# A recurrence whose backward numerator scan runs over pairs of tokens

## The chip, the cores and the metric

The kernel runs on one core of a Trainium2 chip. A core has five engines that each take their instructions in order from a queue of their own: PE (matrix products), DVE (vector operations and scans), ACT (functions of one input), POOL (a second, slower vector engine) and SP, which here only starts transfers. They wait for each other by semaphores. [...] The metric is the device time of one execution in microseconds. The kernel before takes 1098.87 us, the median of 3 runs (1096.25 to 1105.0).

## The reference

Two layers follow each other. The first is a linear attention over 1024 tokens, 1024 channels and 4 batches, run in both directions; the second is a slot attention, which the change leaves alone. The first, cut to what matters:

```
decay = exp(-exp(w)) * (0.5 + 0.5*tf)          # per batch and channel
ek  = exp(min(kf, 30)); ekv = ek * vf          # here k and v are one input
a_t = a_{t-1}*decay + ekv_t                    # forward: nf, df
...                                            # the same backward: nb, db
euk = exp(min(u + kf, 30))
num = nf + nb - ekv + euk*vf
den = df + db - ek + euk
out = sigmoid(r) * (num / max(den, 1e-8)) * (0.8 + 0.2*tf)
```

## The kernel before

Channels lie on the 128 partitions, tokens along the free axis. The recurrence is a loop of 32 passes, one for each batch and block of 128 channels, each over a tile of 128 x 1024. Pass i's numbers are written here as i modulo 4, since four passes share one load of r (`gate`) and one sigmoid over it (L279).

A forward scan followed by a backward scan over its result gives nf + nb - ekv, up to a factor that is put into the inputs. So each pass needs four scans on DVE: forward over `ek` and `ekv`, and backward over each result in place (`scan`, L320). The tile `both` holds denominator and numerator side by side; there are two such tiles, used in turn. The first value of a backward scan (the edge) is made by ACT (`make_edge`, L332).

The order of the work is written out by hand: nearly every instruction is pinned to program order. In pass i DVE runs the two forward scans and the backward scan of the denominator (in `sums_a`), then `den_sum` (L360, adds the own term), `newton` (L419) of pass i-1, `own_value` (L364) and the backward scan of the numerator (`numerator`). Beside it:

- POOL runs `gated` of pass i-1 (L412, L413), `terms` of pass i+1 (L302, L308), `floor` (L381, after `den_sum`) and `product` of pass i-1 (L431, after `newton`). `product` reads the tile `both` of pass i-1, which is also the one that the forward scans of pass i+1 write: they wait for it.
- ACT runs the exponentials (L312, L292), the logarithm and exponential of the quotient (`guess`, L397 and L399), a square (L434), the two edges, and the copies out of the PSUM tile `ptr` (L457, L489, L504).
- PE sums the numerator in PSUM with the sign turned: `add_negated` (L370) multiplies by minus the identity, first the own values `ov`, later the scanned numerator, 2 products each. It also contracts gates and squares for the routing logits (`contract`, L442) and turns pass i-2's tokens in two halves (`turn_half`, L456).

Three passes in four turn tokens in this place (i modulo 4 = 1, 2, 3). From pass 3 on these also do one piece of weight work (`projection`, L488 or L496). In i modulo 4 = 1 and 2 a further half is turned at the end of the pass and copied in the next. All of these share one buffer `ptr`: each use waits until ACT has copied the one before. Passes with i modulo 4 = 0 turn nothing and do no weight work. The PE order of pass i is: first half turned, `contract` of a square, second half turned, `contract`, the weight piece, `add_negated` of `ov`, `contract` of gates of pass i-1, the further half, `add_negated` of the numerator.

The last pass works in halves, and its last steps lie on the way to the top-8 search that opens the second layer.

## Time and profile before

| quantity | us |
|---|---|
| median of 3 runs | 1098.87 |
| profiled execution, whole time | 1097.41 |
| its span, first to last instruction | 1095.6 |
| start of the first and of the last `den_sum` (L360) | 18.6 and 405.9 |
| DVE busy from 38 to 406 us | 366.48 of 368.00 |
| POOL busy in the same stretch | 338.73 |
| PE busy in the same stretch | 300.06 |
| ACT busy in the same stretch | 255.12 |

Mean granted TensorE clock over the span: 0.962. The profile cuts the span into 40 slices of about 27.4 us; the recurrence fills the first 15 of them. In the profile, a line of the timeline gives the start of an instruction or of a row of equal ones, how long it took, its engine, its line in the code, its output and inputs, and in brackets how long the engine had been idle before it and who ended that.

### The profile page before, as it was taken

How to read it: one execution, taken by the hardware profiler on the slowest of the kernel's cores; microseconds unless marked ns; L12 is line 12 of the kernel's file. 1: busy time of each engine (PE TensorE's matmuls, PEld its weight loads, DVE VectorE, ACT ScalarE, POOL GpSimd, SP SyncE). 2: the span in 40 equal slices, each digit the busy share in tenths (PEclk: the TensorE clock that was granted, in tenths of full speed). 3: DMA queues.
4: the chain of work that ended last, by engine and by line, in shares of the span. 5: the costliest groups of instructions: out<-in, count | busy, mean ns of one | idle time of the engine just before them, and what ended most of it. 6: DMA issues, size and time to landing. Idle time of an engine off the chain costs nothing.

```text
span 1095.6 us, 11962 instructions
## 1 busy us (share of the span) xinstructions
PE 972.7 (89%) x4156; PEld 541.9 (49%) x4156; DVE 767.0 (70%) x1049; ACT 507.5 (46%) x787; POOL 546.4 (50%) x417
## 2 busy tenths in 40 slices
PE   2688788877878788899999999998999999999996
PEld 0123222222323233584666666664584676766763
DVE  7999999999999995144666666656144555555555
ACT  5476777768676763012334444444123333333332
POOL 4999999999999882100222222222100444434444
PEclk9789899989989899999999999999999999999999
DMA  8575574856564265790577777553760454545554
GB/s 272 181 261 170 155 225 128 281 153 232 171 212 129 82 200 156 256 355 16 203 277 281 267 253 273 205 200 120 282 260 20 149 216 179 213 188 208 192 210 154
DMA packets 121788, 218.79 MB, mean 200 GB/s; under 512 B 10928, under 2 KB 76592, under 8 KB 121728
## 3 DMA queue, kind: packets, MB, share of 16 engines
q1 hardware_dynamic: 87872, 199.15, 51.3%
q10 hardware_dynamic: 33280, 16.78, 5.3%
q0 software_dynamic: 576, 2.10, 0.5%
q8 instruction: 33, 0.54, 0.2%
q14 instruction: 27, 0.22, 0.1%
HBM read 150.90 MB, written 67.11 MB: 199 GB/s over the span
## 4 chain that ended last, share of the span: by engine, by line
PE 58%; DVE 31%; issue 4%; POOL 3%; ACT 2%; DMA 1%; SPq 0%; POOLq 0%; DVEq 0%; ACTq 0%
DVE both L320 22%; PE psc L1095 20%; PE po L1152 19%; DVE both L419 3%; DVE ov L364 3%; PE ptr L1083 3%; PE pk L955 3%; PE pkv L885 3%; PE pv L1023 2%; PE pet L1141 1%; PE pw L835 1%; PE raw L442 1%; PE poc L1168 1%; PE num L370 1%; PE pmix L817 1%
## 5 line engine op out<-in xcount | busy, mean ns | idle before, releaser
L1095 PE MATMUL psc<-km,xt 128*128 128x272 f32 (+1 forms) x1024 | 238.4, 386 | 0.0
L1152 PE MATMUL po<-vm,e 128*128 128x512 f32 x512 | 230.4, 593 | 0.9 <-ACT e L1142 0.9
L1095 PEld LDWEIGHTS psc<-km,xt 128*128 128x128 f32 x1024 | 189.5, 190 | 29.1
L370 PE MATMUL num<-ov,minus_ident 128*128 128x512 f32 x128 | 88.6, 831 | 97.6 <-DVE ov L364 97.6
L1129 POOL TENSOR_TENSOR e<-e,den 128x256 f32<-128x256 f32 x64 | 40.5, 633 | 252.5 <-DVE den L1127 231.4
L320 DVE TENSOR_TENSOR_SCAN both<-columns,edges,both 128x1024 f32<-128x1024 f32 x64 | 148.2, 2316 | 0.0
L1152 PEld LDWEIGHTS po<-vm,e 128*128 128x128 f32 x512 | 94.8, 190 | 95.7 <-issue 85.4
L1193 DVE SCALAR_TENSOR_TENSOR y<-y,inv,npost_bc 128x1024 f32<-128x1024 f32 x62 | 79.6, 1285 | 41.2 <-POOL inv L1188 41.2
L1161 DVE TENSOR_TENSOR y<-po,y 128x512 f32<-128x512 f32 x128 | 85.8, 674 | 30.9 <-PE po L1152 30.6
L1181 ACT ACTIVATE junk<-y 128x1024 f32<-128x1024 f32 x63 | 66.7, 1058 | 69.2 <-DVE y L1193 69.1
L370 PEld LDWEIGHTS num<-ov,minus_ident 128*128 128x128 f32 x128 | 28.2, 244 | 134.3 <-issue 67.7
L1188 POOL TENSOR_TENSOR inv<-mean,minus_half 128x1 f32<-128x1 f32 x64 | 35.5, 555 | 96.8 <-DVE mean L1186 96.8
L412 POOL TENSOR_TENSOR both<-both,quo 128x1024 f32<-128x1024 f32 (+1 forms) x33 | 75.7, 2295 | 14.9 <-ACT quo L399 14.0
L308 POOL TENSOR_TENSOR ekv<-ek,kf 128x1024 f32<-128x1024 f32 (+1 forms) x33 | 75.6, 2293 | 2.6
L1142 ACT COPY e<-pet 128x256 f32<-128x256 f32 x64 | 23.8, 371 | 113.1 <-PE pet L1141 112.9
L413 POOL TENSOR_TENSOR gate<-gate,quo 128x1024 f32<-128x1024 f32 (+1 forms) x33 | 75.3, 2283 | 0.0
L431 POOL TENSOR_TENSOR gate<-gate,both 128x1024 f32<-128x1024 f32 x31 | 73.3, 2366 | 1.2
L1290 POOL TENSOR_TENSOR y<-y,xin 128x1024 f32<-128x1024 f32 x31 | 73.1, 2358 | 1.4 <-DVE y L1193 1.4
L320 DVE TENSOR_TENSOR_SCAN both<-columns,ek 128x1024 f32<-128x1024 f32 (+1 forms) x32 | 71.5, 2234 | 2.0 <-POOL gate L431 2.0
L320 DVE TENSOR_TENSOR_SCAN both<-columns,ekv 128x1024 f32<-128x1024 f32 (+1 forms) x32 | 71.4, 2231 | 0.0
L442 PE MATMUL raw<-gate,lhs 128*32 128x512 f32 x128 | 69.3, 666 | 0.6 <-POOL gate L431 0.5
L1186 DVE TENSOR_SCALAR mean<-total 128x1 f32<-128x1 f32 x64 | 9.8, 153 | 85.1 <-ACT junk L1181 45.7
(203 smaller groups left out, 1536.9 us busy)
## 6 DMA issues: line engine op xcount, KB each, us to landing
y<-rows SPq DMA_DIRECT2D x64, 512.0 KB, 4.2
kf<-in_ft_dram SPq DMA_DIRECT2D x32, 512.0 KB, 5.3
gate<-in_xt_dram SPq DMA_DIRECT2D x32, 512.0 KB, 6.5
turned_rows<-gate SPq DMA_DIRECT2D x32, 512.0 KB, 3.5
xt<-turned_rows SPq DMA_DIRECT2D x32, 512.0 KB, 5.2
rows<-y SPq DMA_DIRECT2D x32, 512.0 KB, 2.9
xin<-in_x_dram SPq DMA_DIRECT2D x32, 512.0 KB, 4.5
rows<-stage ACTq DMA_DIRECT2D x31, 512.0 KB, 4.4
```

Of the source, the lines that this page charges most:

```text
L308: pin(nc.gpsimd.tensor_tensor(ekv[:, part], ek[:, part], kf[:, part], ALU.mult))
L320: nc.vector.tensor_tensor_scan(dst[:, way], dec, src[:, way], start, ALU.mult, ALU.add)
L370: nc.tensor.matmul(num_ps[:, ts(h, 512)], minus_ident, src[:, ts(h, 512)], start=first, stop=not first,)
L412: pin(nc.gpsimd.tensor_tensor(den, den, quo[:, part], ALU.mult))
L413: pin(nc.gpsimd.tensor_tensor(xk, xk, quo[:, part], ALU.mult))
L431: pin(engine.tensor_tensor(xk, xk, factor[:, part], ALU.mult))
L442: nc.tensor.matmul(raw[rows_b, ts(h, 512)], lhs[:, w].rearrange("p h s -> p (h s)"), src[:, ts(h, 512)], start=(k == 0 and w == k), stop=( ...
L1095: nc.tensor.matmul(psc[g][:, :n], xt_g[g][:, k, :], maps["km"][:, g // NT, k, :n], start=(k == 0), stop=(k == NK - 1),)
L1152: nc.tensor.matmul(po, et[:, ts(c, P)], vm[:, c, ts(h, 512)], start=(c == 0), stop=(c == 1),)
L1161: pin(nc.vector.tensor_add(half, po, half))
L1193: pin(nc.vector.scalar_tensor_tensor(y[g], y[g], inv[g], npost_bc, ALU.mult, ALU.mult))
L1290: pin(nc.gpsimd.tensor_add(y[g - 1], y[g - 1], xin[g - 1]))
```

## The change

The numerator's backward scan runs over 512 pairs where it ran over 1024 tokens. With f the forward result and d the decay, PE makes the pairs f[2s] + d*f[2s+1] in PSUM (2 products, one by a diagonal matrix of d, one by the identity), DVE scans them backward with d*d and writes the even tokens into `both` in place, and PE makes the odd tokens: f[2s+1] + d*y[2s+2]. The own values are written by DVE straight into the PSUM tile `num`, even tokens first, odd ones behind; PE adds three products to it (even tokens, odd f, d times the next even one). The sign is no longer turned; `newton` subtracts the other way round. The pairs use the buffer `ptr`. ACT makes the diagonal matrix of d in each pass. The last pass keeps its backward scan over all tokens, and adds it to `num` in the plain order. The PE order of pass i becomes: first half turned, `contract`, second half turned, `contract`, the weight piece, `make_pairs`, `contract` of gates of pass i-1, the further half, `add_pairs`.

```
-            edge = edges[:, i % 8, :]
+            flat = rec.tile([P, 2 * L + 2], F32, tag="both", bufs=2, name=f"both_{i}")
+            both = flat[:, : 2 * L].rearrange("p (n t) -> p n t", n=2)
+            edge = [edges[:, i % 8, :], flat[:, 2 * L : 2 * L + 1]]
...
+        def parted(tokens, i):
+            return tokens.rearrange("p (s h) -> p h s", h=2) if i < N - 1 else by_half(tokens)
+
+        def by_half(tokens):
+            return tokens.rearrange("p (h s) -> p h s", h=2)
+
         def own_value(i, kf, own):
-            ov = rec.tile([P, L], F32, tag="ov", bufs=1, name=f"ov_{i}")
-            pin(nc.vector.scalar_tensor_tensor(ov, own, EXP_CLAMP, kf, ALU.min, ALU.mult))
-            return ov
-
-        def add_negated(num_ps, src, first, halves=(0, 1)):
...
+            num_ps = rec_ps.tile([P, L], F32, tag="num", bufs=1, name=f"num_{i}")
+            pin(
+                nc.vector.scalar_tensor_tensor(
+                    by_half(num_ps), parted(own, i), EXP_CLAMP, parted(kf, i), ALU.min, ALU.mult
+                )
+            )
+            return num_ps
+
+        def add(num_ps, h, src, by=ident):
+            pin(
+                nc.tensor.matmul(
+                    num_ps[:, ts(h, 512)], by, src, start=False, stop=True, skip_group_check=True
+                )
+            )
...
+        def decay_matrix(i):
+            m = rec.tile([P, P], F32, tag="decay_matrix", bufs=2, name=f"decay_matrix_{i}")
+            pin(nc.scalar.mul(m, ident, decay[:, i // NK, i % NK : i % NK + 1]))
+            return m
+
+        def make_pairs(i, both, by):
+            f = both[:, 1, :].rearrange("p (s h) -> p h s", h=2)
+            pairs = rec_ps.tile([P, 4, P], F32, tag="ptr", bufs=1, name=f"pairs_{i}")
+            pairs = pairs.rearrange("p q c -> p (q c)")
+            pin(nc.tensor.matmul(pairs, by, f[:, 1], start=True, stop=False))
+            pin(nc.tensor.matmul(pairs, ident, f[:, 0], start=False, stop=True))
+            return pairs
+
+        def add_pairs(num_ps, flat, by):
+            f = flat[:, L : 2 * L].rearrange("p (s h) -> p h s", h=2)
+            later = flat[:, L + 2 :].rearrange("p (s h) -> p h s", h=2)[:, 0]
+            add(num_ps, 0, f[:, 0])
+            add(num_ps, 1, f[:, 1])
+            add(num_ps, 1, later, by)
...
-        def numerator(i, both, edge):
-            num = both[:, 1, :]
-            scan(num, num, i, edge[:, 1:2], True)
+        def numerator(i, both, edge, pairs):
+            even = both[:, 1, :].rearrange("p (s h) -> p h s", h=2)[:, 0]
+            dec = decay_2[:, i // NK, i % NK : i % NK + 1].to_broadcast([P, L // 2])
+            pin(
+                nc.vector.tensor_tensor_scan(
+                    even[:, ::-1], dec, pairs[:, ::-1], edge, ALU.mult, ALU.add
+                )
+            )
...
+            if i < N - 1:
+                pairs[i] = make_pairs(i, both[i], by[i])
             if past:
                 gated(i - 1, both[i - 1], quo[i - 1])
...
-            ov = own_value(i, kf[i], own[i])
-            num_ps[i] = rec_ps.tile([P, L], F32, tag="num", bufs=1, name=f"num_{i}")
-            add_negated(num_ps[i], ov, True)
+            num_ps[i] = own_value(i, kf[i], own[i])
             if i == N - 1:
                 break
-            numerator(i, both[i], edge[i])
+            numerator(i, both[i], edge[i], pairs[i])
...
             if past:
                 square(i - 1, quo[i - 1])
+            if i + 1 < N - 1:
+                by[i + 1] = decay_matrix(i + 1)
+            if past:
                 contract(i - 1, gate_of(i - 1), (i - 1) % NK)
...
-            add_negated(num_ps[i], both[i][:, 1, :], False)
+            add_pairs(num_ps[i], flat[i], by[i])
```

More of the change, by code (lines that the diff above doesn't have):

```diff
@@ L228 @@
     plus_half = rc.tile([P, 1], F32, name="plus_half")
-    minus_ident = rc.tile([P, P], F32, name="minus_ident")
+    decay_2 = rc.tile([P, B, NK], F32, name="decay_2")
     nc.scalar.activation(w_sb, w_sb, AF.Exp)
@@ L246 @@
     nc.vector.tensor_scalar_mul(twice_root, twice_root, 2.0)
-    nc.vector.tensor_scalar_mul(minus_ident, ident, -1.0)
     dec_flat = decay.rearrange("p b k -> p (b k)")
+    nc.vector.tensor_tensor(decay_2.rearrange("p b k -> p (b k)"), dec_flat, dec_flat, ALU.mult)
     gap = rc.tile([P, B * NK], F32, name="gap")
@@ L262 @@
         dec_ps = columns[:, : B * NK].rearrange("p (b k) -> p b k", k=NK)
-        edges = rc.tile([P, 8, 2], F32, name="edges")
+        edges = rc.tile([P, 8, 1], F32, name="edges")
         nc.vector.tensor_copy(dec_ps, decay)
@@ L327, in sums_a @@
             b, k = i // NK, i % NK
-            both = rec.tile([P, 2, L], F32, tag="both", bufs=2, name=f"both_{i}")
-            edge = edges[:, i % 8, :]
+            flat = rec.tile([P, 2 * L + 2], F32, tag="both", bufs=2, name=f"both_{i}")
+            both = flat[:, : 2 * L].rearrange("p (n t) -> p n t", n=2)
+            edge = [edges[:, i % 8, :], flat[:, 2 * L : 2 * L + 1]]
             def make_edge(n):
-                pin(nc.scalar.mul(edge[:, n : n + 1], both[:, n, L - 1 : L], turn[:, b, k : k + 1]))
+                pin(nc.scalar.mul(edge[n], both[:, n, L - 1 : L], turn[:, b, k : k + 1]))
             late = i % HK == 1
@@ L354, in sums_a @@
             den = both[:, 0, :]
-            scan(den, den, i, edge[:, 0:1], True)
-            return both, edge
+            scan(den, den, i, edge[0], True)
+            return both, edge[1], flat
         def den_sum(both, own):
@@ L365, in own_value @@
-            return ov
-        def add_negated(num_ps, src, first, halves=(0, 1)):
-            for h in halves:
-                pin(
-                    nc.tensor.matmul(
-                        num_ps[:, ts(h, 512)],
-                        minus_ident,
-                        src[:, ts(h, 512)],
-                        start=first,
-                        stop=not first,
-                    )
-                )
+            num_ps = rec_ps.tile([P, L], F32, tag="num", bufs=1, name=f"num_{i}")
@@ L381, in floor @@
             pin(nc.gpsimd.tensor_scalar(den, den, DEN_MAX, DEN_MIN, ALU.min, ALU.max))
-        def numerator(i, both, edge):
-            num = both[:, 1, :]
-            scan(num, num, i, edge[:, 1:2], True)
+        def numerator(i, both, edge, pairs):
[6 more added lines that the diff above has]
+            )
         def numerator_half(i, both, edge, h):
             num = both[:, 1, ts(h, 512)]
-            scan(num, num, i, edge[:, 1:2] if h else both[:, 1, 512:513], True)
+            scan(num, num, i, edge if h else both[:, 1, 512:513], True)
         def guess(i, both, parts=(every,)):
@@ L417, in newton @@
             b = i // NK
+            den = both[:, 0, part]
+            num = num_ps[:, part]
+            if out is None:
+                den, num = parted(den, i), by_half(num)
             pin(
                 nc.vector.scalar_tensor_tensor(
-                    both[:, 0, part] if out is None else out[:, part],
-                    both[:, 0, part],
+                    den if out is None else out[:, part],
+                    den,
                     twice_root[:, b : b + 1],
-                    num_ps[:, part],
+                    num,
                     ALU.subtract,
                     ALU.mult,
+                    reverse0=True,
                 )
@@ L524 @@
         ek, ekv, both, edge, own, quo, num_ps = {}, {}, {}, {}, {}, {}, {}
+        flat, pairs, by = {}, {}, {}
         halves = [ts(0, 512), ts(1, 512)]
@@ L532 @@
         ekv[0] = terms(0, kf[0], ek[0], halves)
+        num_ps[0] = rec_ps.tile([P, L], F32, tag="num", bufs=1, name="num")
+        for h in range(2):
+            nc.tensor.matmul(
+                num_ps[0][:, ts(h, 512)], ident, logits[:, ts(h, 512)], start=True, stop=True
+            )
+        by[0] = decay_matrix(0)
         late_copy = None
@@ L540 @@
             own[i] = rec_ps.tile([P, L], F32, tag="own", bufs=1, name=f"own_{i}")
-            both[i], edge[i] = sums_a(
+            both[i], edge[i], flat[i] = sums_a(
                 i,
@@ L636 @@
             gated(i, both[i], quo[i], part)
-            add_negated(num_ps[i], both[i][:, 1, :], False, (h,))
+            add(num_ps[i], h, both[i][:, 1, part])
             if n == 0:
@@ L698 @@
                 pin(nc.tensor.transpose(banks[n][:, q, :], block, ident))
-        stage_last = rec.tile([P, 2, L], F32, tag="both", bufs=2, name="stage_last")[:, 0, :]
+        stage_last = rec.tile([P, 2 * L + 2], F32, tag="both", bufs=2, name="stage_last")[:, :L]
         stage_last = stage_last.rearrange("p (t c) -> p t c", c=P)
```

## The prediction

> **What bounds the kernel now.** I read the busy slices of the page first, then the chain that ended last, then the timeline of one period. In the slices, DVE is full in the first 15:

> ```profile
> DVE  7999999999999995144666666656144555555555
> POOL 4999999999999882100222222222100444434444
> PEclk9789899989989899999999999999999999999999
> ```

> The chain in order of time agrees: it runs through DVE scans, one piece of four for each pass, 12.44 to 12.52 us apart:

> ```profile
> 147.75 8.87 DVE both L320 x4
> 160.20 8.87 DVE both L320 x4
> 172.64 8.87 DVE both L320 x4
> ```

> From the first `den_sum` at 18.6 to the last at 405.9 the 31 periods average 12.49. The timeline of the period from 152 shows what the other engines have to spare:

> ```profile
> 152.11 2.26 DVE L320 TENSOR_TENSOR_SCAN both<-columns,ekv 128x1024 f32<-128x1024 f32 x1
> 153.92 0.60 PE L456 MATMUL ptr<-ident,gate 128*128 128x128 f32 x4
> ...
> 154.41 0.29 ACT L332 ACTIVATE edges<-both,turn 128x1 f32<-128x1 f32 x1 [0.97 <-DVE both L320]
> ...
> 157.68 0.58 ACT L489 COPY wp<-pwt 128x512 f32<-128x512 f32 x1 [0.97 <-PE pwt L488]
> 157.79 1.27 DVE L419 SCALAR_TENSOR_TENSOR both<-both,twice_root,num 128x1024 f32<-128x1024 f32 x1
> ...
> 159.15 2.37 POOL L431 TENSOR_TENSOR gate<-gate,both 128x1024 f32<-128x1024 f32 x1
> ...
> 160.11 2.34 DVE L320 TENSOR_TENSOR_SCAN both<-columns,edges,both 128x1024 f32<-128x1024 f32 x1
> ...
> 160.25 3.45 PE L370 MATMUL num<-ov,minus_ident 128*128 128x512 f32 x4 [2.61 <-DVE ov L364]
> ```

> To be seen: DVE never pauses; the buffer `ptr` is free again at 158.26, only 1.85 before the numerator's scan at 160.11; POOL needs 11.63 for its six steps (L412 starts at 149.90 and at 161.53, no pause between); PE stands still before L370, and then its four records take 3.45 where 1.98 is usual.

> **DVE's own work.** From 160.11 to 172.56 the starts give 2.26 + 2.18 + 2.18 + 2.36 for the scans, then 1.14, 1.19, 1.14: 12.45. The numerator's scan falls to 512 elements; the one row of such a backward scan is 1283 ns, less the 0.09 by which DVE's instructions overlap: 1.20, so -1.06. `own_value` now writes the tile that `newton` just read and must wait for its end: 1.30 in place of 1.19, +0.11. Writing PSUM costs 756 ns in the 512-wide L419 of the last pass, against 692 in L671 of the same shape into SBUF: +0.07. DVE would need 12.45 - 1.06 + 0.18 = 11.57. With nothing else late, 31 periods give 27 us.

> The pairs come from PSUM, which no scan's data did; the 1283 ns row already reads its decay there, and I keep 1.20 (bounds 1.20 to 1.35, 0 to 5 us in all). `own_value`, `newton` and the scan now step over every second element. No row does. Their contiguous forms cost 1.14 to 1.20, and doubled they would add 1.1 each. [...] `own` lies in PSUM. [...]

> ACT's new diagonal matrix is like the 128x128 copy of L514, 0.27 us. It stands after the square, ahead of the next edge, for which ACT waits 0.29 to 1.31 in the rows of L332; ACT has 113 of 368 us idle. Nothing; uncovered it is 8 us. `decay_2` and two zeroing products before the loop hide in PE's and DVE's waits for the first loads. No transfer is added or moved on SP, ACT or POOL.

> **POOL's handover.** `product` frees the tile that the next forward scan writes. From the start of `newton`: 1.27, 2.37 and two hand-overs of 0.04 are 3.72; DVE's own way is 1.30 + 1.21 + 1.20 = 3.71. Just even. POOL's 11.63 is a floor of its own, 0.06 above DVE.

> **The new wait: pairs.** The numerator's scan now waits for `make_pairs`, and the next three DVE scans and `den_sum` are queued behind it; POOL's `floor` waits for those. Let E be the end of the forward scan over `ekv`. DVE comes to the numerator at E + 5.74 now (154.37 to 160.11), after at E + 5.92. PE's chain in a turning pass, from the start of its first half, by the rows from 153.92: ACT's last copy out of `ptr` ends 4.34 later (158.26). Then two 512-wide products, 0.955 apart (1.91), and 0.15 for the last one's end and the hand-overs: 6.40.

> When does that first half start? Call N the start of the numerator's scan in the pass before and s the time it was late. `newton` ends 1.24 before N - s, so `product` ends at N + 1.17 - s. PE waits for it, then contracts gates (1.83), turns the further half if there is one (0.58), and adds three products (2.87, one more than now): N + 5.87 - s, or 6.45 - s. E is N + 5.65. So the scan is late by s' = 0.70 - s, or 1.28 - s, and never under 0.1, as ACT cannot copy before the edge at E + 0.3. For i modulo 4 = 1, 2, 3 (the further half lies before 2 and 3): 0.70, 0.58, 0.70. In the fourth pass the pairs are ready at N + 9 against 11.57: none. Four periods are 4 x 11.57 + 1.98 + 0.1 (POOL) = 48.36 against 49.8; 7.75 such groups give -11.2. The four passes with the longer weight piece (1.17 for 0.65, with a copy of 0.37 for 0.58) give +1.3. So -9.9 at full PE clock.

> **The clock.** In the pass without turning, PE is done at N + 9, and has nothing until `product` ends at N + 12.8: idle for 3.8. Before, it stands still here too (2.6 to 5.0), but then only added to a tile that nobody needed for 9 us. The stretches from 115 to 170 show what follows (columns: PE, PEld, DVE, ACT, POOL busy, then the granted clock):

> ```profile
> 118.90:122.20 3.30, 0.00 (x0) 0.00 (x0) 3.27 (x4) 3.27 (x4) 3.00 (x3) 1.00 0.00 0
> 122.30:125.70 3.40, 2.76 (x4) 1.18 (x4) 3.40 (x3) 3.37 (x4) 3.39 (x2) 0.50 0.20 53
> 125.80:129.10 3.30, 3.30 (x5) 0.53 (x4) 3.30 (x2) 1.46 (x3) 3.30 (x3) 0.50 0.96 256
> 156.40:159.80 3.40, 1.24 (x6) 0.42 (x4) 3.37 (x4) 1.54 (x3) 3.37 (x3) 1.00 1.01 370
> 159.80:163.20 3.40, 2.95 (x4) 1.17 (x4) 3.40 (x3) 3.37 (x4) 3.38 (x2) 0.51 1.10 356
> ```

> A stretch of 3.4 us with PE busy for only 1.24 is followed by half clock; one with 2.76 of 3.40 does not end it. [...] By the rows, 1.24 us of work do not save a window, and nearly every such pass goes to half clock. [...] Half clock then lasts 2.9 to 6.3 us of the work that follows (one or two windows, less what lies in the idle time), of which half is lost: 1.5 to 3.1, middle 2.3. That work is the contraction, the three products and the first turned half, straight ahead of the pairs of i modulo 4 = 1. So s = 0.70 + 2.3 = 3.0 there; in the next pass PE has room (0.1), then 1.28 - 0.1 = 1.2: 4.3 for 2.0. Seven groups: +16.1.

> **The end.** In the last pass two products of `ov` at half clock (3.44 us at 409.46) stood on the chain; they are gone, but the first half scan ends at 410.6 and PE still has its two others to do: -1.5.

> **The sum.** -9.9 + 16.1 - 1.5 = +4.7. The profiled execution took 1097.41 (span 1095.6): 1102.1. The median is 1.5 above that execution: 1104.

> **The rivals.** (A) Faster: PE keeps its clock, or its lateness is absorbed. For it: PE stood still for 2.2 us before 147.81 and for 1.5 before 185.21 and kept its clock. Against: 3.8 is longer than both, and 2.6 before 160.25 lost it. -11.4 in all, 1087; and were the pairs never late at all, 27 us and 1072. (B) Slower, by one mechanism: half clock lasts three windows, up to the pairs of the pass after. Place: i modulo 4 = 1, seven times. It decides once the window behind the first has PE busy for under some 2.8 of 3.4; the waits on `ptr` leave such holes. Three windows are 10.2, half lost 5.1 in place of 2.3: 2.8 x 7 = +20, so 1124. For it: two windows at 122.3 in the trace. Against: the three added products fill the second window. (C) Slower: the step of two in PSUM doubles `own_value`: 1138.

> **How the numbers follow.** Chances: forecast 0.43, A 0.22, B 0.25, C 0.10. The forecast's own range is 1098 to 1111 (0.8 us of lost clock either way times seven, and 1 to 2 for the scan's bounds). The range from 1085 to 1125 cuts off half of A and most of C. A change of 1% (11 us) is about what a measurement of this kernel can tell from none. Faster: 0.17 of A. Slower: B, C and 0.04 of the forecast, 0.39. Within: 0.44.

> **What would show it.** The numerator's scan at about 1.28 and its start late on PE's pairs, by about 3 us every fourth pass; periods of 11.6 elsewhere; half clock at each i modulo 4 = 0. Wrong, if no stall stands before that scan, if it is near 2.3, or if `own_value` or `newton` grow by half a microsecond.

## The result, and the profile after

The changed kernel takes 1106.68 us (median of 20 runs, 1103.21 to 1113.58), the kernel before 1098.24 (20 runs, 1095.6 to 1105.0): ratio 1.0079, 95% interval 1.0061 to 1.0097. It is slower by 0.8%. The forecast was 1104, within 1%.

The profiled execution has a span of 1107.1 us, 11.5 more than before. Of these, 9.55 lie in the recurrence (first to last `den_sum`: 18.04 to 414.86, 396.82 for 387.27), which began 0.56 earlier. From the last `den_sum` to the first copy of the raw logits the time is 14.98 for 15.24. The other 2.7 lie in the second layer, which the change leaves alone: in this execution a stretch of half clock from 454.3 to 461.1 falls on it, and 2.64 of the 2.7 arise between 456 and 466. Such stretches lie elsewhere in other executions (from 436.2 on in e10, at 437.9 and 492.5 in e1), so the medians' 8.4 is the better size.

The same three rows of the page's slices, for the kernel after:

```profile
DVE  7898898989898986233666656565233555555555
POOL 4999898989898972200222222222100343444444
PEclk9899898989899899899999999999999999999999
```

DVE was full in nearly each of the first 15 slices; now every second one has a hole. The granted clock dips in about every second slice too. The timeline of DVE in a quiet pass and the pass after it:

```profile
224.51 1.23 DVE L374 SCALAR_TENSOR_TENSOR num<-own,kf 128x1024 f32<-128x1024 f32 x1
225.65 1.27 DVE L417 TENSOR_TENSOR_SCAN both<-decay,both,pairs 128x512 f32<-128x512 f32 x1
226.96 2.29 DVE L320 TENSOR_TENSOR_SCAN both<-columns,ek 128x1024 f32<-128x1024 f32 x1
...
234.91 1.27 DVE L458 SCALAR_TENSOR_TENSOR both<-both,twice_root,num 128x1024 f32<-128x1024 f32 x1
236.22 1.23 DVE L374 SCALAR_TENSOR_TENSOR num<-own,kf 128x1024 f32<-128x1024 f32 x1
240.80 1.28 DVE L417 TENSOR_TENSOR_SCAN both<-decay,both,pairs 128x512 f32<-128x512 f32 x1 [3.35 <-ACT quo L434]
```

The scan is 1.27 for 2.34, `own_value` 1.23, and the quiet pass (numerator of i modulo 4 = 0, at 225.65) has no hole. In i modulo 4 = 1 DVE stands still for 3.35. The bracket names ACT's L434, but the chain of waits in order of time gives the true releaser, PE's pairs:

```profile
226.97 3.62 PE raw L482 x4
230.60 3.79 PE num L382 x6
234.39 0.44 PE ptr L496 x4
...
238.62 1.17 PE pairs L398 x2
239.79 0.92 PE pairs L399 x2
240.71 0.03 issue
240.73 0.02 DVEq L417
240.75 0.05 issue
240.80 1.28 DVE both L417
```

So the path to the end leaves DVE and runs through PE, with one copy on ACT in between, for nearly 14 us. Four stretches of the windows view around it (columns as in the prediction: PE, PEld, DVE, ACT, POOL busy, then the granted clock, DMA share, GB/s) show why the two first steps take 3.62 and 3.79:

```profile
222.20:225.60 3.40, 0.54 (x2) 0.00 (x0) 3.37 (x3) 3.29 (x4) 2.41 (x3) 1.00 0.01 2
225.60:229.00 3.40, 2.02 (x3) 0.54 (x4) 3.37 (x3) 3.37 (x5) 3.39 (x2) 0.50 0.29 95
229.00:232.40 3.40, 3.40 (x5) 0.83 (x3) 3.40 (x3) 1.66 (x4) 3.40 (x3) 0.50 0.72 214
232.40:235.80 3.40, 3.40 (x12) 1.29 (x11) 3.30 (x3) 0.59 (x1) 3.32 (x3) 1.00 0.00 0
```

PE has 0.54 us of work in the first stretch, and the next two are granted half the clock: 6.83 us. That is two windows of 3.413: within the span, each stretch of half clock in this trace is one or two of these long. This repeats: between 100 and 400 us half clock begins at 123.2, 174.4, 225.6, 276.8, 328.0 and 379.2, once in four passes, and lasts 6.83 each time (in the group before these it begins at 75.4 and lasts 3.41). The periods (from one `den_sum` to the next, by the i modulo 4 = 1, 2, 3, 0 of the numerator's scan between them) are 15.0, 11.66, 12.80 and 11.71, where the prediction's formula has 14.6, 11.7, 12.8 and 11.67.

### The profile page after: what moved, and what is told of

It is laid out like the page before. It is cut to its first block, busy times and chain, and to the rows that moved or that the text cites. A ratio compares the mean times of both kernels' runs of the same rounds, so it can differ in the third digit from the quotient of the medians.

```text
span 1107.1 us, 12203 instructions
## 1 busy us (share of the span) xinstructions
PE 1002.8 (91%) x4218; PEld 552.3 (50%) x4218; DVE 739.5 (67%) x1049; ACT 516.7 (47%) x818; POOL 549.2 (50%) x417
## 4 chain that ended last, share of the span: by engine, by line
PE 74%; DVE 12%; POOL 7%; ACT 3%; issue 2%; DMA 1%; SPq 1%; POOLq 0%; DVEq 0%; ACTq 0%
PE psc L1146 20%; PE po L1203 19%; DVE both L320 8%; PE raw L482 7%; PE num L382 4%; POOL gate L471 3%; PE ptr L1134 3%; PE pk L1006 3%; PE pkv L936 3%; PE pv L1074 2%; PE ptr L496 2%; DVE both L417 2%; PE pairs L398 2%; PE pw L886 1%; POOL both L411 1%
## 5 line engine op out<-in xcount | busy, mean ns | idle before, releaser
L482 PE MATMUL raw<-gate,lhs 128*32 128x512 f32 x128 | 74.7, 712 | 47.9 <-POOL gate L471 47.8
L447 POOL TENSOR_TENSOR both<-both,quo 128x1024 f32<-128x1024 f32 (+1 forms) x33 | 76.1, 2305 | 21.7 <-ACT quo L434 21.2
L382 PE MATMUL num<-both,ident 128*128 128x512 f32 x128 | 73.8, 702 | 6.3 <-DVE both L320 4.3
L320 DVE TENSOR_TENSOR_SCAN both<-columns,edges,both 128x1024 f32<-128x1024 f32 x32 | 74.4, 2325 | 1.8 <-ACT edges L333 1.8
L320 DVE TENSOR_TENSOR_SCAN both<-columns,ek 128x1024 f32<-128x1024 f32 (+1 forms) x32 | 71.8, 2243 | 3.5 <-POOL gate L471 3.3
L320 DVE TENSOR_TENSOR_SCAN both<-columns,ekv 128x1024 f32<-128x1024 f32 (+1 forms) x32 | 71.4, 2231 | 0.0
L1137 ACT COPY xt<-ptr 128x512 f32<-128x512 f32 x64 | 37.0, 577 | 70.2 <-PE ptr L1134 70.2
```

The lines of the kernel that those rows point to most:

```text
L320: nc.vector.tensor_tensor_scan(dst[:, way], dec, src[:, way], start, ALU.mult, ALU.add)
L382: nc.tensor.matmul(num_ps[:, ts(h, 512)], by, src, start=False, stop=True, skip_group_check=True)
L447: pin(nc.gpsimd.tensor_tensor(den, den, quo[:, part], ALU.mult))
L482: nc.tensor.matmul(raw[rows_b, ts(h, 512)], lhs[:, w].rearrange("p h s -> p (h s)"), src[:, ts(h, 512)], start=(k == 0 and w == k), stop=( ...
```

## The experiments

Each kernel ran beside the kernel before on the same chip (medians of 1096.75 to 1098.28 there). Products of a zero matrix (`nothing`), added to an open sum, keep PE busy and change no value.

| kernel | median us | ratio to before, 95% |
|---|---|---|
| changed kernel | 1106.68 | 1.0061 to 1.0097 |
| e1: + 3 filling products | 1092.47 | 0.9909 to 0.9963 |
| e2: + 1 filling product | 1097.47 | 0.9975 to 1.0020 |
| e3: before + 3 filling products | 1098.67 | 0.9984 to 1.0026 |
| e4: no pairs, scan from SBUF | 1105.30 | 1.0044 to 1.0109 |
| e5: own values in PSUM alone | 1101.51 | 1.0015 to 1.0048 |
| e6: e1, one weight piece moved | 1092.02 | 0.9923 to 0.9963 |
| e7: no pairs, decay from PSUM | 1094.46 | 0.9950 to 0.9980 |
| e8: e1, no weight pieces | 1084.25 | 0.9827 to 0.9905 |
| e9: e1, pairs made but not read, in place | 1093.20 | 0.9923 to 0.9963 |
| e10: e6 + 4 filling products at the end | 1093.91 | 0.9946 to 0.9992 |
| e11: e1 + one product ahead of each turn | 1105.01 | 1.0030 to 1.0100 |
| e12: e9, scan into a tile of its own | 1081.40 | 0.9796 to 0.9893 |

### The clock: filling products

```
+        def keep_busy(i, n):
+            b = i // NK
+            for _ in range(n):
+                pin(nc.tensor.matmul(raw[32 * b : 32 * b + 32, :512], nothing, npost_bc[:, :512],
+                    start=False, stop=False, skip_group_check=True))
...
                 pairs[i] = make_pairs(i, both[i], by[i])
+            if i >= HK and i % HK == 0:
+                keep_busy(i - 1, 3)
```

> The changed kernel with three more 128x512 products (weights of zeros, added to the routing sums, so nothing changes in the result) behind make_pairs in each pass with i modulo 4 = 0. Theory clock (half clock after PE's idle time makes the pairs of the next pass late): the idle time falls from 4.2 to about 1.4 us, no half clock in the loop, the pass with i modulo 4 = 1 falls from 15.0 to about 12.3 us, and the whole to 1086 to 1092 us, some 8 to 10 us faster than the kernel before. Rival handshake (the buffer ptr and the longer PE chain alone make the pairs late): nothing gained, 1105 to 1110 us. Rival memory step (stepping over every second element slows DVE): nothing gained either.

Measured: 1092.47, at the upper end of the first range and 14.2 less than the changed kernel. No half clock is left between 42 and 400 us, and the recurrence takes 380.24 for 396.82. The four periods are 12.34, 12.19, 12.32 and 11.72. DVE's waits from 38 us to the end of the recurrence, by the waits view (us in all, times, the longest), first of the changed kernel:

```profile
DVE both L417 <- ACT quo L434: 30.2, 13, 3.5
DVE both L320 <- POOL gate L471: 3.3, 2, 2.9
DVE both L417 <- PE pairs L399: 2.1, 2, 1.1
```

and of the kernel with the three products:

```profile
DVE both L420 <- PE pairs L402: 15.1, 20, 2.0
DVE both L323 <- POOL gate L474: 3.3, 2, 2.9
DVE both L420 <- ACT quo L437: 1.4, 1, 1.4
```

The wait ahead of the numerator's scan falls from 32.3 to 16.5: half of it was the clock. Work that computes nothing made the kernel faster, and faster than the kernel before.

One product in place of three:

> The same with one product in place of three (0.9 us of work, about 3.3 us of idle time left). By the rows of the trace before (a window of 3.4 us with 1.24 us of work is followed by half clock): half clock stays in every such pass, 1103 to 1109 us. [...]

Measured: 1097.47, under the range. Starts of the numerator's scan in five of the passes:

```profile
234.92 1.28 DVE L420 TENSOR_TENSOR_SCAN both<-decay,both,pairs 128x512 f32<-128x512 f32 x1 [2.30 <-ACT quo L437]
246.48 1.28 DVE L420 TENSOR_TENSOR_SCAN both<-decay,both,pairs 128x512 f32<-128x512 f32 x1
259.38 1.28 DVE L420 TENSOR_TENSOR_SCAN both<-decay,both,pairs 128x512 f32<-128x512 f32 x1 [1.20 <-ACT quo L437]
270.89 1.27 DVE L420 TENSOR_TENSOR_SCAN both<-decay,both,pairs 128x512 f32<-128x512 f32 x1
286.10 1.28 DVE L420 TENSOR_TENSOR_SCAN both<-decay,both,pairs 128x512 f32<-128x512 f32 x1 [3.41 <-ACT quo L437]
```

In two groups of the profiled execution the clock held (stalls of 0.74), in two it fell for one window (2.3 to 2.5), in three for two windows (3.4 to 3.5). So half clock did not stay in every such pass, and it did not go from every one: the same product in the same place gave 0, 1 and 2 windows. That it depends on where a window begins would explain this; no run moves the windows alone.

The same products in the kernel before, where PE also stood still and lost its clock, but nobody waited for it:

> The kernel before with the same three products in the passes with i modulo 4 = 0. Theory: there DVE sets the time and nobody waits for PE, so half clock costs nothing and its absence brings nothing: 1096 to 1101 us, periods 12.45 us as before. If half clock cost the kernel before anything, it would be faster by more than 3 us.

Measured: 1098.67, periods of 12.44 as before. The products stand in one pass of four, and PE has holes in the others too: half clock between 60 and 406 us falls from 58.0 to 40.5 us. So this run doesn't show the kernel before at full clock throughout, but a third of its half clock taken away brought nothing. The gain of e1 thus isn't a gain of filling as such; it needs PE on the path.

### What is left once the clock is kept: the wait for pairs

PE's lateness itself, made larger by one product in each pass ahead of a turn:

```
             add_pairs(num_ps[i], flat[i], by[i])
+            if i >= HK and i % HK < 3:
+                keep_busy(i - 1, 1)
```

> The changed kernel with the three filling products, and one more 128x512 product of PE (0.955 us, zero weights) behind the three additions of the passes 0, 1 and 2 modulo 4, that is ahead of each turned half: the cost of PE's lateness by itself. Theory (lateness s' = c - s in turn, c now 1.6, 2.2, 2.2): stalls of 1.6, 0.6 and 1.6 in place of 0.7, 0.6, 0.7, so +1.8 a group, +13 in all against the three filling products alone (1092): 1103 to 1107. Rival (linear, each product costs its whole time): +2.9 a group, +20: 1112. Rival (PE's additions are covered): 1092 to 1094.

Measured: 1105.01, inside the first range. But the stalls in a group are 1.86, 0.96, 1.46 and 0, for 1.6, 0.6, 1.6 and 0 expected: 4.3 for 3.8. Against e1's 2.0 that is 2.3 more, midway between the 1.8 of the theory and the 2.9 of the linear rival, and in the profiled executions the recurrence grew by 16.1 (380.25 to 396.35), midway between 13 and 20. In these two executions the rest was shorter than in e1, by 2.2 at the end and by 6.1 in the second layer, so the whole time says less here than the recurrence. A product of 0.955 thus costs less than its time, some 0.8 of it. That a late scan lets PE start earlier relative to it in the pass after would explain the direction; the formula's size isn't borne out.

Then pairs without anyone waiting for them. The odd tokens are left out here, and decay squared is read from PSUM:

```
-                    even[:, ::-1], dec, pairs[:, ::-1], edge, ALU.mult, ALU.add
+                    even[:, ::-1], dec, even[:, ::-1], edge, ALU.mult, ALU.add
```

> The changed kernel with the three filling products, and pairs made by PE as before, but the numerator's scan does not read them: it reads the even tokens with decay squared held in PSUM, and the odd tokens are left out. PE has the same work as with the filling products alone, so its clock is the same; only DVE's wait for the pairs is gone. Theory (what is left of the loss beside the clock is that wait): passes of 11.65 to 11.8, no idle time ahead of the numerator's scan, 1076 to 1083 us. Rival (PE is late by other ways too, as where no pairs were made at all: its copies out of PSUM hold up ACT, and with it POOL and the product): passes stay at 12.1 or more, 1088 or above.

Measured: 1093.20, with much the same stalls as e1:

```profile
231.22 1.28 DVE L422 TENSOR_TENSOR_SCAN both<-columns,both 128x512 f32<-128x512 f32 x1 [0.74 <-PE pairs L404]
```

This doesn't speak for the rival. The line names the pairs still: the scan writes in place over even tokens that the pairs' products read, so it has to wait for PE though it doesn't use the result. The edit had not removed the wait. Written into a tile of its own (`loose`, from which PE adds; the odd tokens left out again):

```
-                    even[:, ::-1], dec, even[:, ::-1], edge, ALU.mult, ALU.add
+                    loose[:, ::-1], dec, even[:, ::-1], edge, ALU.mult, ALU.add
...
-            add(num_ps, 0, f[:, 0])
+            add(num_ps, 0, loose)
```

> The run before wrote the scan in place, over tokens that the pairs' products read, so the scan still waited for PE (0.74 us of idle time ahead of it, as before). Here the scan writes a tile of its own, from which PE then adds; the pairs are made and not read, the odd tokens are left out, and the three filling products are kept. Theory (what is left beside the clock is the scan's wait for PE's pairs): no idle time ahead of the numerator's scan, passes of 11.65 to 11.8, 1076 to 1083 us. Rival (PE's lateness reaches DVE the other way too: its copies out of PSUM stand on ACT ahead of the first guess, POOL's product comes late, and the forward scan over ek waits for it): the idle time moves to that scan, passes stay at 12.1 or more, 1088 or above.

Measured: 1081.40, and no idle time ahead of the numerator's scan in any pass. PE does the same products as in e1. All that DVE waits for from 38 to 400 us, by the waits view (the second line is the last pass):

```profile
DVE both L325 <- POOL gate L478: 6.3, 9, 2.9
DVE num L465 <- PE num L387: 3.6, 1, 3.6
```

The passes are 11.7, except 12.1 in i modulo 4 = 1, where the scan over `ek` waits some 0.5 for POOL's product: the rival's mechanism is there, at 0.4 for every four passes. The recurrence takes 368.67. So the parts are, by profiled executions: 396.82 after, less 16.6 for the clock (e1), less 11.6 more for the wait (e12), against 387.27 before. DVE's shorter work alone is worth -18.6.

### Ways around the wait

Without the pairs, the odd tokens left out, and no filling:

```
-                    even[:, ::-1], dec, pairs[:, ::-1], edge, ALU.mult, ALU.add
+                    even[:, ::-1], dec, even[:, ::-1], edge, ALU.mult, ALU.add
...
-                pairs[i] = make_pairs(i, both[i], by[i])
+                pairs[i] = None
```

> The changed kernel without make_pairs: the numerator's scan reads the even tokens where it read the pairs, so the odd tokens are left out of the numerator. It shows what DVE's shorter work is worth with nothing to wait for. Theory (the wait for the pairs is what takes the gain back): all passes at POOL's 11.65 us, 31 times 0.8 us less, 1072 to 1076 us. Rival: another wait (product, floor, edges) or slower new DVE forms hold the loop back, over 1085 us.

A miss: 1105.30 where 1072 to 1076 was expected. By the groups of 200 to 300 us, DVE's scan and POOL's step beside it:

```profile
L417 DVE TENSOR_TENSOR_SCAN both<-decay,both 128x512 f32<-128x512 f32 x8 | 18.8, 2348 | 0.0
L447 POOL TENSOR_TENSOR both<-both,quo 128x1024 f32<-128x1024 f32 x8 | 22.6, 2819 | 3.4 <-ACT quo L434 3.4
```

The scan of 512 takes 2.35 where that with pairs takes 1.28. Either the step of two or its operands did it; every scan so far had one operand in PSUM, and this one has none (of the recurrence's tiles, the kernel puts `columns`, `own` and those that PE writes into PSUM, the others into SBUF). So the same with decay squared in PSUM:

```
+        dec_2_ps = columns[:, B * NK : 2 * B * NK].rearrange("p (b k) -> p b k", k=NK)
+        nc.vector.tensor_copy(dec_2_ps, decay_2)
...
-            dec = decay_2[:, i // NK, i % NK : i % NK + 1].to_broadcast([P, L // 2])
+            dec = dec_2_ps[:, i // NK, i % NK : i % NK + 1].to_broadcast([P, L // 2])
```

> Again without make_pairs (odd tokens left out of the numerator), but the scan's decay now comes from PSUM, as in the other scans, and only its data from SBUF. Theory (in the run without pairs two SBUF operands made the scan 2.4 us instead of 1.28, and the wait for pairs is what takes the gain back): scan 1.28 us, all passes 11.65 us, 1072 to 1078 us. Rival (the scan is slow for its step over every second element): 2.4 us again, passes of 12.6 us, 1103 to 1107 us.

```profile
L419 DVE TENSOR_TENSOR_SCAN both<-columns,both 128x512 f32<-128x512 f32 x8 | 10.2, 1274 | 0.5 <-ACT both L335 0.5
L449 POOL TENSOR_TENSOR both<-both,quo 128x1024 f32<-128x1024 f32 x9 | 21.4, 2376 | 7.6 <-ACT quo L436 7.3
```

The scan is back at 1.27: not the step of two, but where the operands lie. And not that alone. The first such scan of e4 took 1.27 too; it and a later one, with POOL's steps beside them:

```profile
18.88 1.04 POOL L411 TENSOR_SCALAR both<-both 128x1024 f32<-128x1024 f32 x1 [2.23 <-DVE both L361]
19.76 1.27 DVE L417 TENSOR_TENSOR_SCAN both<-decay,both 128x512 f32<-128x512 f32 x1
...
187.44 2.36 POOL L471 TENSOR_TENSOR gate<-gate,both 128x1024 f32<-128x1024 f32 x1
188.53 2.35 DVE L417 TENSOR_TENSOR_SCAN both<-decay,both 128x512 f32<-128x512 f32 x1
189.79 3.26 POOL L447 TENSOR_TENSOR both<-both,quo 128x1024 f32<-128x1024 f32 x1
```

At 19.76 POOL is done after 0.16. The other 30 scans of e4 start under a TENSOR_TENSOR step of POOL, and each ends 1.08 to 1.09 after that step, whether it took 1.82 in all or 2.99. In turn POOL's L447, where it starts under the scan, ends 2.14 to 2.19 after it in 24 of 25 cases. So the scan isn't slow by itself: in e4, where both its operands lie in SBUF, it took 1.27 beside no step of POOL's and mostly 2.35 beside one, and POOL's step 2.82 for e7's 2.38. In e7 the scan takes 1.27 to 1.28 under the same steps. The time of e7, 1094.46, is between both ranges, since passes take mostly 11.8 to 12.7. The waits view names another way from PE to DVE:

```profile
ACT stage L499 <- PE ptr L498: 60.4, 48, 3.3
...
POOL both L449 <- ACT quo L436: 22.5, 20, 2.6
DVE both L322 <- POOL gate L473: 15.7, 20, 2.8
```

ACT's copies out of `ptr` stand ahead of `guess` in its queue. With PE late they are late, then `gated` on POOL, then `product`, and the scan over `ek` waits for that. With less work PE is at half clock more often here than in the changed kernel (17 stretches between 60 and 410 us, for 7). Since e12 keeps the clock and has 11.7 in most passes, with the pairs' products on PE as well, this second way seems to weigh mostly while PE is slow.

The own values alone, without pairs:

```
-            return tokens.rearrange("p (s h) -> p h s", h=2) if i < N - 1 else by_half(tokens)
+            return by_half(tokens)
...
-            numerator(i, both[i], edge[i], pairs[i])
+            scan(both[i][:, 1, :], both[i][:, 1, :], i, edge[i], True)
...
-            add_pairs(num_ps[i], flat[i], by[i])
+            for h in range(2):
+                add(num_ps[i], h, both[i][:, 1, ts(h, 512)])
```

> One part of the change alone: own values written straight into PSUM, two identity products added to them, the numerator's scan over all 1024 tokens as before. Theory: DVE still sets the time and pays the wait for newton's end, 0.11 us, and 0.01 for the write, so passes of 12.57 us, 1100 to 1104 us. Rival (the products of ov on PE cost something before): faster than 1096 us.

Measured: 1101.51, periods of 12.57 in place of 12.44. Writing the own values into PSUM costs 0.12 in each pass, and PE's two saved products give nothing. All that the change gains comes from the shorter scan.

Without the weight pieces (the routing weights of the second layer are zero here), on top of e1:

```
-        projection.append(group_sums)
+        projection.clear()
+        nc.vector.memset(wo_cw.rearrange("p j s -> p (j s)"), 0.0)
```

> The changed kernel with the three filling products and without the weight pieces (the weight work of the second layer's routing is left out, its weights are zero). Theory: at full clock what is left of the lateness is PE's chain through the buffer ptr, of which the piece is 1.3 us; without it the passes fall from about 12.3 to 11.65 to 11.8 us, and the whole to 1076 to 1083 us. Rival (the three added products and the contraction alone make the pairs late): passes stay at 12.1 us or more, over 1087 us.

Measured: 1084.25, 8.2 less than e1 (6.9 of it in the recurrence of the profiled executions). Most passes are 11.7, those of i modulo 4 = 1 12.1, and three are 13.0 to 13.1, each behind a window of half clock; PE has less work here, and the three filling products do not hold the clock everywhere, which would account for a time a little above the range. The pieces, where they stand, thus cost some 7 to 8 us. One piece moved to where PE has room:

```
-            if i >= 3 and i % HK and projection:
+            if i >= 3 and i % HK > 1 and projection:
...
             h = i % HK - 1
+            if i >= HK and h == -1 and projection:
+                late_copy = projection.pop(0)()
```

> The changed kernel with the three filling products, and with the weight piece of each pass with i modulo 4 = 1 moved to the end of the pass before, where its copy out of ptr is made as the late ones are. Theory: pass i modulo 4 = 1 loses its lateness of 0.7 us, the next one has 1.2 us in place of 0.5, since it is no longer helped by the first one's, and the third next to nothing: some 0.5 us less for each group of four, 1086 to 1091 us, 8 to 12 us faster than the kernel before. Rival (the sum of PE's work in the three passes is the limit, wherever a piece stands): as with the filling alone, 1091 to 1095 us.

Measured: 1092.02 for e1's 1092.47, no difference, as the rival had it. The periods are 12.04, 12.80, 11.73 and 11.72 for 12.34, 12.19, 12.32 and 11.72. The scan's wait of i modulo 4 = 1 is gone, and that of 2 is 1.2. This is the formula s' = 1.28 - s again, now with s = 0: what one pass gives up, the next takes.

Last, filling at the end of the recurrence, on top of e6:

```
             num_ps[i] = own_value(i, kf[i], own[i])
             if i == N - 1:
+                keep_busy(i - 1, 4)
```

> The changed kernel with the three filling products and the moved piece, and four more filling products in the last pass, behind the own values, so that the last additions run at full clock. Theory (the half clock at the last additions stands on the path to the end): 1 to 3 us less than without the four, 1089 to 1091. Rival (PE's last additions are not what is late there): 1092 or more.

PE's timeline behind the last scans, of e6:

```profile
403.88 2.07 PE L385 MATMUL num<-both,ident 128*128 128x512 f32 x2 [4.71 <-DVE both L323]
405.89 1.92 PE L485 MATMUL raw<-gate,lhs 128*32 128x512 f32 x2
407.74 1.21 PE L385 MATMUL num<-both,ident 128*128 128x512 f32 x2
```

and of e10, with the four products ahead of them:

```profile
403.48 1.13 PE L385 MATMUL num<-both,ident 128*128 128x512 f32 x2 [0.73 <-DVE both L323]
404.54 1.05 PE L485 MATMUL raw<-gate,lhs 128*32 128x512 f32 x2
405.51 1.12 PE L385 MATMUL num<-both,ident 128*128 128x512 f32 x2
```

The last additions do run at full clock, and the time from the last `den_sum` to the first copy of the raw logits falls from 15.28 to 13.38. But the median is 1093.91, not less. In the profiled executions the rest of the kernel took 674.4 in e6 and 680.8 in e10, and a half clock of 10.2 from 436.2 on lies in the latter; nearly all of the difference arises by 451. It doesn't come each time: three of e10's twelve executions had a mean granted clock of 0.990 to 0.992 and took 1088.5 to 1088.6, the nine others 0.972 to 0.984 and 1093.0 to 1100.6. Whether the filling makes the half clock more frequent stays open; the local gain is shown, a gain of the whole is not.

The fastest kernels that compute everything are e1 and e6, at 1092: 0.6% under the kernel before.

## Why the prediction was right, and where it was off

**DVE's own work.** 11.57 was forecast, 11.67 with POOL's hand-over. Quiet passes are 11.71. The scan's 1.27 (1.28 forecast) and `own_value`'s wait for `newton` (start to start 1.31, 1.30 forecast) hold; writing PSUM costs 0.01 (1.232 for 1.218), not 0.07. The lines view from 38 to 406 us, before and after:

```profile
L364 DVE SCALAR_TENSOR_TENSOR ov<-own,kf 128x1024 f32<-128x1024 f32 x29 | 35.3, 1218 | 0.0
L374 DVE SCALAR_TENSOR_TENSOR num<-own,kf 128x1024 f32<-128x1024 f32 x29 | 35.7, 1232 | 1.0
```

The second steps over every other element of `own` in PSUM and takes 1232 ns for 1218. That this doubles the time, as in rival C, was an assumption which no run shows, and C falls.

**The wait for pairs.** Right in form, and in size in this kernel. In after, from the start of the first half turned (234.22) to the scan (240.80) are 6.58, for 6.40. At full clock (e1, the six full groups from i = 5 on) the stalls are 0.74 to 0.86, 0.41 to 0.90, 0.49 to 0.86 and 0, for 0.70, 0.58, 0.70 and 0. e11 bears out the alternation c - s (long, short, long) but not its size: with c = 2.2, stalls of 0.3 and 1.2 would have followed 1.86 and 0.96, and 0.96 and 1.46 did.

**The clock.** This decided the sign, and the step taken from the rows was right: half clock follows the quiet pass in each of the six groups from 123 us on, behind a stretch of 3.4 us with 0.49 to 0.60 us of PE work, and without it the kernel is 14.2 faster (e1). Somewhat larger than forecast was the term "middle 2.3" of lost time: `raw` took 3.62 for 1.90 and `num` 2.95 for 1.96, together 2.7, inside the bounds of 1.5 to 3.1. PE's idle time before it was 4.23, for 3.8. With these the stalls of a group are 3.35, 0, 1.21 and 0: 4.6 for 4.3. Four periods are 51.2 for 50.7.

**The end.** -1.5 was forecast, -0.26 measured: the two products of `ov` are gone, but a half clock from 420.2 to 423.6 lies on the last additions. With the clock kept there, in e10, this stretch takes 13.38, so the half clock is worth 1.6 here. The step took the products' time off and kept no account of the clock behind it.

**The sum.** Of +6.2 forecast for the recurrence the profiled execution has +9.55. By e1 the lost clock is 16.6 of this, for 16.1, and the rest -7.0 for -9.9. So the larger miss is the part at full clock: the first five periods gained nothing in e1 (63.4 for 63.3) and 0.3 in the changed kernel, where an even sum over 31 passes counts 1.8. With the end (+1.2 against its forecast), the earlier start (-0.56) and the second layer (+2.7, in no sum) this makes +11.5 for +4.7. The total is what is left of two large terms of opposite sign, so its nearness to the forecast, within 0.3%, says little of either: e1 shows the clock's term, the other was 2.9 off, and the half clock in the second layer is chance.

**ACT's matrix** takes 0.39 (0.27 forecast). No run takes it away by itself, and no row shows a wait that it causes.

**The rivals.** A (clock kept) gave 1087; e1, whose clock is kept from 42 to 400 us, is at 1092. In its profiled execution the recurrence is 7.0 shorter than before, for -9.9; the end, with half clock from 400.3, is 0.3 longer, for -1.5; and the second layer, with half clock at 437.9 and 492.5, is 5.8 longer. B (three windows) didn't occur in the later groups: the second window has 3.40 of 3.40 us of PE work, above its deciding point of 2.8. "Were the pairs never late" gave 1072; e12, with the clock kept, has 1081. The 27 us of DVE's work are 18.6 there. In the last 26 passes most periods are 11.70 for 12.44, 0.74 in place of 0.88, and six are 12.09 for 12.44 because of the wait for `product`: -17.0 in all. The five periods ahead of these give only -1.6; one of them is bound by POOL in both kernels (14.58 before, 14.47 in e12), which the prediction's even sum over 31 passes left out.

The expected gain thus went into two waits: for PE's clock and, behind it, for PE's chain of turning, copying and pairs. Neither engine's busy share showed it, as PE was at 300 of 368 us.

## What to carry to other kernels

When work moves from a full engine to one that has room on average, ask which of its results the full engine will now wait for in the same pass, and at which clock: idle time that hurt nobody before becomes a price as soon as the work behind it is on the path (the three products took 14.2 us off the changed kernel in e1, and nothing off the one before in e3). If a trace shows half clock behind a hole of PE's ahead of such work (here 6.83 us of it behind a hole of 4.23), a few products that compute nothing are a cheap test of what the clock costs, and sometimes the remedy. An experiment that stops reading a result has not removed the wait for it while the reader writes over the producer's operands (0.74 us of it was left in e9).

## What the runs showed of the hardware

**A lock.** 15 windows are 51.20 us, and four of the changed kernel's passes took 51.14 to 51.30 from 95 us on (49.8 before, 48.5 to 48.7 in e1). The late pass stretches the group to just the length at which the hole meets the same window again, and all six groups from 123 us on lost the clock for exactly two windows. In e2 the last three groups did the same, at 51.18 to 51.27. Whether the groups are drawn to this length or met it by chance, no run tests.

**DVE and POOL at SBUF.** A scan of 512 with both data operands in SBUF took 1.27 us where POOL was idle (one case, e4). Started under a TENSOR_TENSOR step of POOL it ended 1.08 to 1.09 after that step (30 cases), mostly 2.35 in all, and POOL's next step averaged 2.82 for 2.38. With one operand in PSUM the scan took 1.27 to 1.28 under the same steps (e7).
